# A graph network layer on one core: layer norm's centring on ScalarE and its scale at the split of h, in PSUM

## The chip, the core and the metric

The kernel runs on one core of a Trainium2 chip. TensorE (PE in the profile, its weight loads PEld) multiplies matrices and writes to PSUM. VectorE (DVE) and ScalarE (ACT) work element by element on SBUF and PSUM. GpSimd (POOL) here issues the indirect DMAs that scatter rows to memory, and SyncE's queue (SP) issues the other DMAs. The engines run on their own and wait for each other through semaphores. The metric is the device time of one execution in microseconds.

## What is computed

12,500 nodes with 128 features, 412,500 edges sorted by destination. The reference, cut to what matters:

```python
def ssp(x): return softplus(x) - LOG2
hn  = maximum(layernorm(x), 0)                 # (x - mean) / sqrt(var + 1e-5), then relu
h   = hn @ W_in2f                              # 12500 x 128
Wij = (ssp(f_ij @ W_f1 + b_f1) @ W_f2 + b_f2) * rcut_ij[:, None]
agg = segment_sum(h[dst] * Wij, src, 12500)    # one row an edge
out = x + ssp(agg @ W_o1 + b_o1) @ W_o2 + b_o2
```

Layer norm has no weights. Its scale 1/sqrt(var) is positive, one number a node, so it may be applied before the relu, after it, or after the product with W_in2f: relu(s·c) @ W = s·(relu(c) @ W).

## The kernel before, in words

**Edges.** The edges run in 806 chunks of 512, one chunk a step of the main loop (`for k in range(-3, ...)`, line 1200; `step`, line 989). In a step PE, ACT and DVE work on several chunks in different phases: the filter network (PE `hidden` line 682, ACT Abs, Exp and Ln on lines 691 to 694, DVE line 700, all for two chunks at once every second step, then PE `value` line 797 onto a bias that ACT writes to PSUM, line 789); the gather of h rows (a DMA of a window of h into `near`, a DVE comparison line 776, PE `pick` line 808, ACT `picked` line 818, which multiplies by the edge weight); the row number of each message in its destination table (DVE lines 705 and 729, PE lines 724 and 757); the message itself (DVE line 826). GpSimd then scatters the four 128-row tiles of the message to `slots` (line 830).

**Pace.** `behind` (line 586) ties PE's work of a chunk to the landing of the scatters of eight chunks before, and the message tile `o` has eight buffers.

**Quads of nodes.** h is made by `make_h` (line 327), 512 nodes (a quad, four 128-row tiles) at a time, 25 quads, 98 tiles. It is a generator: each `yield` ends what it emits into one step. The first two quads run ahead of the loop. `side` (line 1158) starts one of the other 23 every nine steps from about step 6 on, so they take about the first 210 of the 806 steps. Counted from a quad's start, these are its ticks:

- 0: the load of x into `xb`; 3: DVE statistics (lines 338, 339), ACT Ln and Exp for the scale `rs` (342, 343)
- 4: DVE four small operations that sharpen `rs` (347 to 351), then DVE centres and scales each tile of `xb` (line 354, four instructions)
- 5: PE transposes to PSUM (359), ACT relu to `xT` (361)
- 6: PE multiplies by W_in2f into the PSUM tile `hps` (365), ACT rounds it to bf16 (367, one instruction)
- 7: DVE subtracts the rounded part into the SBUF tile `left` (370), ACT rounds the rest (371)
- 8: DVE subtracts again (373): h is kept as three bf16 parts. SP stores them to memory (379, 388).

`xps` and `hps` share one PSUM bank (tag `acc`, one buffer). What a step of the loop issues comes ahead of what the quad's tick issues on every engine's queue.

**The output.** x is loaded again for the residual, and the output bias `bo2` (with W_o2's share of b_o1 in it, line 321) is added early: `x_ahead` (line 1092) does this for 14 quads on DVE from step 300 on (`x_early`) and for the other 11 on GpSimd near the end (`x_late`), both through `x_bias` (line 423). `rest` (line 1139) prepares late constants beside the quads and ends with `late_biases`. `count_ps` (line 550) is a PSUM tile with the numbers 0 to 127, which DVE compares with on lines 705 and 882.

Of the kernel before, what the change touches and what calls it, by code (L numbers as in the profile page):

```python
# [9 lines left out]
F32 = mybir.dt.float32  # L10
# [3 lines left out]
AF = mybir.ActivationFunctionType  # L14
ALU = mybir.AluOpType
PSUM = bass.MemoryType.PSUM

P = 128
TG = 16
CH = 512  # L20
NCHUNK = TG * P // CH
QT = CH // P
# [21 lines left out]
def gnn_kernel(  # L44
# [20 lines left out]
    nc = tc.nc  # L65
# [52 lines left out]
    def sbuf(name, shape, dtype=F32):  # L118
        return const.tile(shape, dtype, name=name)

    def spread(t, n):
        return t[:, None, :].to_broadcast([t.shape[0], n, P])
# [13 lines left out]
    for c in range(NC):  # L136
        n = c * CH * N // n_edges
# [6 lines left out]
    bf2, bo2 = (sbuf(n, [P, P]) for n in ("bf2", "bo2"))  # L144
# [20 lines left out]
    ln = ctx.enter_context(tc.tile_pool(name="ln", bufs=2))  # L165
# [150 lines left out]
    def late_biases(psum):  # L316

        nc.vector.tensor_scalar(nbo1, bo1, -1.0, None, op0=ALU.mult)
        b12 = psum.tile([P, QT, P], F32, name="b12_out", tag="acc")[:, 0, :]
        nc.tensor.matmul(b12, bo1.to_broadcast([P, P]), wo2, start=True, stop=True)  # L320
        nc.vector.tensor_add(bo2, b12, bo2)
# [5 lines left out]
    def make_h(q, psum):  # L327

        n = min(QT, NTILE - q * QT)
        xb = early.pop(q, None)  # L330
        if xb is None:
            xb = load_x(q)
            for _ in range(3):
                yield
        st = ln.tile([P, QT, 6], F32, name="st")
        mv = ln.tile([P, QT, 2], F32, name="mv")
        for i in range(n):
            nc.vector.bn_stats(st[:, i, :], xb[:, i, :])
            nc.vector.bn_aggr(mv[:, i, :], st[:, i, :])

        rs = ln.tile([P, QT], F32, name="rs")
        nc.scalar.activation(rs[:, :n], mv[:, :n, 1], AF.Ln, bias=eps)
        nc.scalar.activation(rs[:, :n], rs[:, :n], AF.Exp, scale=-0.5)
        yield

        ve = ln.tile([P, QT], F32, name="ve")
        nc.vector.tensor_scalar(ve[:, :n], mv[:, :n, 1], EPS, -0.5, op0=ALU.add, op1=ALU.mult)
        r2 = ln.tile([P, QT], F32, name="r2")
        nc.vector.tensor_mul(r2[:, :n], rs[:, :n], rs[:, :n])
        nc.vector.tensor_mul(r2[:, :n], r2[:, :n], ve[:, :n])  # L350
        nc.vector.scalar_tensor_tensor(rs[:, :n], r2[:, :n], 1.5, rs[:, :n],
                                       op0=ALU.add, op1=ALU.mult)
        for i in range(n):
            nc.vector.tensor_scalar(xb[:, i, :], xb[:, i, :], mv[:, i, 0:1], rs[:, i:i + 1],
                                    op0=ALU.subtract, op1=ALU.mult)
        yield
        xps = psum.tile([P, QT, P], F32, name="xps", tag="acc")
        for i in range(n):
            nc.tensor.transpose(xps[:, i, :], xb[:, i, :], ident)
        xT = ln.tile([P, QT, P], F32, name="xT")  # L360
        nc.scalar.activation(xT[:, :n, :], xps[:, :n, :], AF.Relu)
        yield
        hps = psum.tile([P, QT, P], F32, name="hps", tag="acc")
        for i in range(n):
            nc.tensor.matmul(hps[:, i, :], xT[:, i, :], win, start=True, stop=True)
        hb = ln.tile([P, QT, 3, P], BF16, name="hb")
        nc.scalar.activation(hb[:, :n, 0, :], hps[:, :n, :], AF.Copy)
        yield
        left = ln.tile([P, QT, P], F32, name="left")
        nc.vector.tensor_sub(left[:, :n, :], hps[:, :n, :], hb[:, :n, 0, :])  # L370
        nc.scalar.activation(hb[:, :n, 1, :], left[:, :n, :], AF.Copy)
        yield
        nc.vector.tensor_sub(hb[:, :n, 2, :], left[:, :n, :], hb[:, :n, 1, :])
        for (b, rows), table in zip(tables, h3_t):
            lo = max(0, b - q * QN) // P
            hi = min(n, (b + rows - q * QN) // P)
            if lo < hi:
                r = q * QN + lo * P - b
                nc.sync.dma_start(
                    table[r:r + (hi - lo) * P, :].rearrange("(c p) f -> p c f", p=P),  # L380
                    hb[:, lo:hi, :, :].rearrange("p c k f -> p c (k f)"))
                if b + rows == QN:
                    yield
            if q == NQ - 1:
                for r in range(NTILE * P - b, rows, P):
                    if r >= 0:
                        nc.sync.dma_start(table[r:r + P, :], none)
        nc.sync.dma_start(
            h3[q * QN:q * QN + n * P, :].rearrange("(c p) f -> p c f", p=P),
            hb[:, :n, :, :].rearrange("p c k f -> p c (k f)"))  # L390
        yield
# [15 lines left out]
    def x_pieces(t0, n):  # L407

        n0 = t0 * P
        full = min(n, N // P - t0)  # L410
        rest = N - n0 - full * P if full < n else 0
        pieces = []
        if full:
            pieces.append((P, slice(0, full), slice(n0, n0 + full * P)))
        if rest:
            pieces.append((rest, slice(full, n), slice(n0 + full * P, N)))
        return pieces
# [2 lines left out]
        for p, cs, rows in pieces:  # L420
            nc.sync.dma_start(xo[:p, cs, :], x[rows, :].rearrange("(c p) f -> p c f", p=p))

    def x_bias(xo, pieces, engine=nc.vector):
        for p, cs, rows in pieces:
            xi = xo[:p, cs, :]
            engine.tensor_add(xi, xi, spread(bo2[:p, :], xi.shape[1]))

    def finish(t0, n, sT, quad, psum, z, xo=None, bank=("v", 3)):

# [108 lines left out]
    with tc.tile_pool(name="edge", bufs=2) as edge, tc.tile_pool(  # L538
        name="quad", bufs=3
# [7 lines left out]
        free_v = free.rearrange("p (t b) -> p t b", b=NBLK)  # L547


        count_ps = state_ps.tile([P, P], F32, name="count_ps")  # L550

        def clear(seg):

# [497 lines left out]
        t0, i = 0, 0  # L1051
        while i < len(segs):

            j = max(range(i, len(segs)), key=lambda j: sum(todo[i:j + 1]) / (due[j] - t0))
            n = sum(todo[i:j + 1])
            for m in range(n):
                zeros.setdefault(t0 + m * (due[j] - t0) // n, []).append(clears.pop(0))
            t0, i = due[j], j + 1
# [5 lines left out]
        while len(rate) < len(at):  # L1064
            n = len(at) - len(rate)
# [13 lines left out]
        i, k = 0, todo[0][0]  # L1079
# [9 lines left out]
                if todo[i - 1][1].ends(todo[i - 1][2]):  # L1089
                    break  # L1090

        def x_ahead(homes, engine):

            pending = []
            for q, xo in homes:
                n = min(QT, NTILE - q * QT)
                pieces = x_pieces(q * QT, n)
                x_load(xo, pieces)
                xs[q] = xo
                pending.append((xo, pieces))  # L1100
                yield
                yield
                if len(pending) > 2:
                    x_bias(*pending.pop(0), engine)
            for w in pending:
                yield
                x_bias(*w, engine)

        def as_quad(t):
            return t.rearrange("p (c f) -> p c f", f=P)  # L1110
# [4 lines left out]
        def early_homes():  # L1115
            for q in range(NX):
                if q < 6:
                    yield q, quad.tile([P, QT, P], F32, name="xo", bufs=6)
                elif q < 12:
                    yield q, ln.tile([P, QT, P], F32, name="xo", tag=("xb", "xT", "left")[q // 2 - 3],  # L1120
                                     bufs=2)
                else:
                    t = ln.tile([P, QT, 3, P], BF16, name="xo", tag="hb", bufs=2)
                    yield q, as_quad(t.rearrange("p c k f -> p (c k f)")[:, :2 * CH].bitcast(F32))

        def late_homes():
            t = None
            for q in range(NX, NQ):
                i = (q - NX) % 2
                if i == 0:  # L1130
                    if q < NX + 8:
                        t = edge.tile([P, NCHUNK, CH], BF16, name="xr", tag="rel", bufs=4)
                        t = t.rearrange("p c e -> p (c e)").bitcast(F32)
                    else:
                        t = edge.tile([P, NB, CH], F32, name="xf", tag="f")
                        t = t.rearrange("p b e -> p (b e)")
                yield q, as_quad(t[:, i * CH:(i + 1) * CH])

        def rest():

            first_load(1)
            part_load(1)
            late_loads()
            yield from bounds(1, nc.vector)
            shift(1)
            for k in range(1, NPART):
                relative(k)
                if k + 1 < NPART:
                    part_load(k + 1)
                yield  # L1150
                yield
                rel_store(k)
                for _ in range(4):
                    yield
            yield from ranges(psum)
            late_biases(psum)

        def side():

# [11 lines left out]
        with tc.manual_schedule():  # L1171
# [23 lines left out]
            bs[0] = groups[0].bias(0)  # L1195
            group(1)
            aside = side()
            x_early = x_ahead(early_homes(), nc.vector)
            x_late = x_ahead(late_homes(), nc.gpsimd)
            for k in range(-3, max(NCH, max(units) + 1)):  # L1200
                for seg, d in zeros.get(k, ()):
                    seg.clears.append(nc.sync.dma_start(*d).ins.name)
# [34 lines left out]
            for q in range(NQ):  # L1237
                n = min(QT, NTILE - q * QT)
# [12 lines left out]
            q = 0  # L1251
# [19 lines left out]
    with tc.If(missed > 0):  # L1271
        with tc.tile_pool(name="any_e", bufs=2) as edge, tc.tile_pool(
            name="any_q", bufs=2
# [51 lines left out]
```

## Time and profile before

| | us |
|---|---|
| median of 4 runs | 5391.92 (5375.06 to 5407.1) |
| the profiled execution | 5360.8, its span 5359.0 |
| DVE busy on line 354 (98 instructions) | 27.6 |
| DVE busy on line 370 / 373 (25 each) | 16.9 / 16.7 |
| ACT busy on line 367 / 371 (25 each) | 14.6 / 15.3 |
| DVE busy on line 426, early additions (14) | 9.5 |
| POOL idle ahead of line 830, whole span | 2109.7 |

A row of the table of groups gives the line, the engine, the operation, output and inputs by the program's names, the shapes and the count, then busy time, the mean of one in ns, and the idle time of the engine just before these instructions with what ended it. "remote" there is a semaphore whose sender the profile can't name; "issue" is a wait for nothing that it shows. The rows of instructions that overlap count the overlap twice in the mean.

### The profile page before, as it was taken

To read this page: it belongs to the slowest core of one execution; us is meant where nothing else is said; L and a number is where in the kernel's file an instruction comes from. 1 tells how busy PE (TensorE), PEld (TensorE's weight loads), DVE (VectorE), ACT (ScalarE), POOL (GpSimd) and SP (SyncE) were. 2 spreads that over 40 slices of the span, in tenths; PEclk is the share of its full clock that TensorE was granted. 3 is DMA by queue.
4 is the path that set the end of the run, shared out by engine and by line. 5 is a ranking of instruction groups with operands and counts; after the bars stand their busy time and mean duration, and the time that the engine had idled before them with its cause. 6 is when DMAs were issued, how large, how long until landed. Compare 5 with 4: busy or idle time off the path is not lost. (4 is left out here: it accounts for less than half of the span.)

```text
span 5359.0 us, 74346 instructions
## 1 busy us (share of the span) xinstructions
PE 3738.0 (70%) x21598; PEld 2866.6 (53%) x21598; DVE 3138.8 (59%) x7101; ACT 2788.0 (52%) x5464; POOL 3148.8 (59%) x3292
## 2 busy tenths in 40 slices
PE   6555655555655555588888888877887777777768
PEld 3343434333433333366666666666666666666657
DVE  5555555555444444466666666666666666666657
ACT  5555555555555555555555555555454554544433
POOL 4666666666666666666666665665565665555552
PEclk8666666666666666688888888888887888888889
DMA  5445444444433334355556555566555655565546
GB/s 150 143 144 148 140 133 141 134 124 134 115 99 99 94 107 143 116 171 180 171 180 214 165 167 166 165 185 197 169 171 156 209 180 147 170 187 152 149 123 190
DMA packets 515221, 820.65 MB, mean 153 GB/s; under 512 B 177188, under 2 KB 312728, under 8 KB 514812
## 3 DMA queue, kind: packets, MB, share of 16 engines
q1 hardware_dynamic: 411212, 602.55, 39.1%
q0 software_dynamic: 103168, 213.15, 11.9%
q8 instruction: 180, 2.95, 0.2%
q14 instruction: 229, 1.88, 0.1%
q10 hardware_dynamic: 432, 0.13, 0.0%
HBM read 419.75 MB, written 395.69 MB: 152 GB/s over the span
## 5 line engine op out<-in xcount | busy, mean ns | idle before, releaser
L830 POOL DMA_INDIRECT slots<-o,slot x3224 | 3111.0, 965 | 2109.7 <-DVE o L826 1228.8
L818 ACT ACTIVATE hg<-picked,rcut 128x128 f32<-128x128 f32 x3224 | 915.2, 366 | 1398.0 <-remote 752.5
L903 PEld LDWEIGHTS acc<-to,m 128*128 128x128 f32 x8152 | 1211.4, 229 | 541.3 <-issue 386.6
L903 PE MATMUL acc<-to,m 128*128 128x128 f32 x8152 | 1320.2, 320 | 254.5 <-issue 165.0
L797 PEld LDWEIGHTS v<-wf,r 128*128 128x128 f32 x6448 | 1090.6, 250 | 389.1 <-issue 262.2
L797 PE MATMUL v<-wf,r 128*128 128x128 f32 x6448 | 1183.5, 340 | 128.4 <-ACT v L789 64.9
L826 DVE TENSOR_TENSOR o<-v,hg 128x512 f32<-128x512 f32 x806 | 553.1, 686 | 1000.2 <-remote 535.4
L682 PE MATMUL z<-f,wf 20*128 20x512 f32 x1612 | 625.1, 854 | 462.5 <-DVE r L700 265.2
L882 DVE TENSOR_TENSOR to<-count_ps,m 128x640 f32<-128x640 f32 (+3 forms) x793 | 637.8, 827 | 294.2 <-remote 114.1
L789 ACT ACTIVATE v<-bf 128x512 f32<-128x512 f32 x804 | 485.0, 603 | 456.7 <-DVE o L826 265.3
L729 DVE TENSOR_REDUCE top<-free 128x4 f32<-128x392 f32 x806 | 449.2, 557 | 457.4 <-remote 309.2
L808 PE MATMUL picked<-near,at 96*128 96x128 bf16 x3224 | 391.3, 256 | 374.5 <-DVE o L826 280.6
L757 PE MATMUL free<-inb,rest_of 128*128 128x392 f16 x806 | 329.7, 409 | 363.6 <-issue 224.8
L700 DVE SCALAR_TENSOR_TENSOR r<-z,nbf,a 128x1024 f32<-128x1024 f32 x403 | 514.2, 1276 | 103.1 <-issue 63.8
L691 ACT ACTIVATE a<-z,bf 128x1024 f32<-128x1024 f32 x403 | 445.9, 1106 | 230.0 <-remote 108.0
L808 PEld LDWEIGHTS <-at 96*128 96x128 bf16 x3224 | 312.1, 118 | 433.8 <-issue 404.9
L682 PEld LDWEIGHTS z<-f,wf 20*128 20x128 f32 x1612 | 156.6, 234 | 672.3 <-DVE r L700 357.8
L694 ACT ACTIVATE a<-a,half 128x1024 f32<-128x1024 f32 x403 | 463.2, 1149 | 13.2
L705 DVE TENSOR_TENSOR inb<-count_ps,blk 128x392 f16<-128x392 f32 x806 | 446.1, 554 | 0.0
L692 ACT ACTIVATE a<-a 128x1024 f32<-128x1024 f32 x403 | 426.3, 1058 | 12.8
L724 PE MATMUL free<-inb,after 128*128 128x392 f16 x806 | 331.3, 411 | 8.2 <-issue 4.4
L724 PEld LDWEIGHTS <-after 128*128 128x128 f16 x806 | 91.5, 114 | 370.7 <-issue 366.5
(115 smaller groups left out, 1428.2 us busy)
## 6 DMA issues: line engine op xcount, KB each, us to landing
m<-slots SPq DMA_DIRECT2D x307, 387.0 KB
m<-slots SPq DMA_DIRECT2D x278, 322.5 KB
rel<-rel_d SPq DMA_DIRECT2D x202, 384.0 KB
slots<-o,slot POOLq DMA_INDIRECT x3224
m<-slots SPq DMA_DIRECT2D x193, 258.0 KB
slots<-zero SPq DMA_DIRECT2D x96, 387.0 KB
f<-in_f_t SPq DMA_DIRECT2D x404, 80.0 KB
slots<-zero SPq DMA_DIRECT2D x58, 516.0 KB
```

The lines of the kernel that those rows point to most:

```text
L682: mm = nc.tensor.matmul(z[:, k, :], wf1[rows, :], self.f[rows, :], start=True, stop=True)
L694: nc.scalar.activation(a, a, AF.Ln, bias=half, scale=0.5)
L700: nc.vector.scalar_tensor_tensor(r, z, nbf1, a, op0=ALU.max, op1=ALU.add)
L729: nc.vector.tensor_reduce(self.top[:, c * QT:(c + 1) * QT], free_v, axis=mybir.AxisListType.X, op=ALU.max)
L789: nc.scalar.activation(v, spread(bf12, QT), AF.Copy)
L797: mm = nc.tensor.matmul(v[:, i, :], r[:, i * P:(i + 1) * P], wf2, start=False, stop=True, skip_group_check=True)
L808: mm = nc.tensor.matmul(ps[:, i, :], at[:, i * P:(i + 1) * P], near, start=i == 0, stop=i == QT - 1, skip_group_check=True)
L818: nc.scalar.activation(hg[:, i, :], ps[:, i, :], AF.Copy, scale=self.rcut[:, j:j + 1])
L826: nc.vector.tensor_mul(o[:, :, :P], v, hg)
L830: put = nc.gpsimd.indirect_dma_start(out=views[j % VIEWS], out_offset=bass.IndirectOffsetOnAxis(ap=self.slot[:, j:j + 1], axis=0), in_=o[: ...
L882: nc.vector.tensor_tensor(to[:, :n, :], count_ps[:, None, :].to_broadcast([P, n, P]), m[:, :n, P:].to_broadcast([P, n, P]), op=ALU.is_equal)
L903: nc.tensor.matmul(self.acc[b // QT][:, i, :], m[:, j, :P], to[:, j, :], start=t == 0, stop=t == self.seg.tiles(b) - 1)
```

## The change

From the third quad on (`q > 1`) four things differ in `make_h`. DVE writes the negated means to a small tile `nm`, and ACT centres each tile of `xb` with an Identity activation whose bias is `nm`; DVE's centring and scaling on line 354 is left out. The product is then without the scale. ACT rounds each tile of `hps` on its own with the scale `rs` as a per-partition operand, four instructions for one. DVE multiplies each tile of `hps` by `rs` and subtracts the rounded part in one instruction, four for one, in place in PSUM. For all quads `left` is gone: the remainder stays in `hps`, and ACT and DVE read it from there.

The PSUM tile of `count_ps` grows to 512 columns and holds a copy of `bo2` beside the numbers, which ACT writes once at the end of `rest`. The early additions of the bias on DVE read that copy; the late ones on GpSimd read `bo2` in SBUF as before.

```diff
         ve = ln.tile([P, QT], F32, name="ve")
+        if q > 1:
+            nm = ln.tile([P, QT], F32, name="nm")
+            nc.vector.tensor_scalar(nm[:, :n], mv[:, :n, 0], -1.0, None, op0=ALU.mult)
+            for i in range(n):
+                nc.scalar.activation(xb[:, i, :], xb[:, i, :], AF.Identity, bias=nm[:, i:i + 1])
         nc.vector.tensor_scalar(ve[:, :n], mv[:, :n, 1], EPS, -0.5, op0=ALU.add, op1=ALU.mult)
...
-        for i in range(n):
+        for i in range(n if q < 2 else 0):
             nc.vector.tensor_scalar(xb[:, i, :], xb[:, i, :], mv[:, i, 0:1], rs[:, i:i + 1],
                                     op0=ALU.subtract, op1=ALU.mult)
...
-        nc.scalar.activation(hb[:, :n, 0, :], hps[:, :n, :], AF.Copy)
+        if q < 2:
+            nc.scalar.activation(hb[:, :n, 0, :], hps[:, :n, :], AF.Copy)
+            yield
+            nc.vector.tensor_sub(hps[:, :n, :], hps[:, :n, :], hb[:, :n, 0, :])
+        else:
+            for i in range(n):
+                nc.scalar.activation(hb[:, i, 0, :], hps[:, i, :], AF.Copy, scale=rs[:, i:i + 1])
+            yield
+            for i in range(n):
+                nc.vector.scalar_tensor_tensor(hps[:, i, :], hps[:, i, :], rs[:, i:i + 1],
+                                               hb[:, i, 0, :], op0=ALU.mult, op1=ALU.subtract)
+        nc.scalar.activation(hb[:, :n, 1, :], hps[:, :n, :], AF.Copy)
         yield
-        left = ln.tile([P, QT, P], F32, name="left")
-        nc.vector.tensor_sub(left[:, :n, :], hps[:, :n, :], hb[:, :n, 0, :])
-        nc.scalar.activation(hb[:, :n, 1, :], left[:, :n, :], AF.Copy)
-        yield
-        nc.vector.tensor_sub(hb[:, :n, 2, :], left[:, :n, :], hb[:, :n, 1, :])
+        nc.vector.tensor_sub(hb[:, :n, 2, :], hps[:, :n, :], hb[:, :n, 1, :])
...
-    def x_bias(xo, pieces, engine=nc.vector):
+    def x_bias(xo, pieces, engine=nc.vector, b=bo2):
...
-            engine.tensor_add(xi, xi, spread(bo2[:p, :], xi.shape[1]))
+            engine.tensor_add(xi, xi, spread(b[:p, :], xi.shape[1]))
...
-        count_ps = state_ps.tile([P, P], F32, name="count_ps")
+        numbers = state_ps.tile([P, CH], F32, name="numbers")
+        count_ps, bo2_ps = numbers[:, :P], numbers[:, P:2 * P]
...
             late_biases(psum)
+            nc.scalar.activation(bo2_ps, bo2, AF.Copy)
...
-            x_early = x_ahead(early_homes(), nc.vector)
-            x_late = x_ahead(late_homes(), nc.gpsimd)
+            x_early = x_ahead(early_homes(), nc.vector, bo2_ps)
+            x_late = x_ahead(late_homes(), nc.gpsimd, bo2)
```

`x_ahead` takes `b` and hands it to `x_bias`.

More of the change, by code (lines that the diff above doesn't have):

```diff
@@ L1090, in gnn_kernel, with x_ahead @@
                     break
-        def x_ahead(homes, engine):
+        def x_ahead(homes, engine, b):
             pending = []
@@ L1103, in x_ahead @@
                 if len(pending) > 2:
-                    x_bias(*pending.pop(0), engine)
+                    x_bias(*pending.pop(0), engine, b)
             for w in pending:
                 yield
-                x_bias(*w, engine)
+                x_bias(*w, engine, b)
         def as_quad(t):
```

## The prediction

> **What bounds the kernel now.** I read the page first, then the engines' busy time by stretches, the waits and the time line of single quads. The page:
>
> ```profile
> span 5359.0 us, 74346 instructions
> PE 3738.0 (70%) x21598; PEld 2866.6 (53%) x21598; DVE 3138.8 (59%) x7101; ACT 2788.0 (52%) x5464; POOL 3148.8 (59%) x3292
> POOL 4666666666666666666666665665565665555552
> ```
>
> No engine is full, and GpSimd is at six tenths from end to end: the kernel is a ring. A chunk's scatters must land before PE works on the chunk eight further on, that work makes a message, and the message starts the next scatters. What the changed part costs is read from stretches: with quads, after them and before the first collection of `slots`, and the long second part.
>
> ```profile
> 150.00:1350.00 1200.00, 679.90 (x3304) 470.79 (x3301) 645.14 (x1737) 670.69 (x1342) 735.35 (x760) 0.66 0.46 138
> 1450.00:1900.00 450.00, 261.22 (x1156) 172.52 (x1156) 202.30 (x481) 243.97 (x471) 280.11 (x292) 0.62 0.34 95
> ```
>
> Columns: stretch, length, busy us (instructions) of PE, PEld, DVE, ACT and POOL, granted clock, DMA share, GB/s. POOL issues four scatters a step: 760/4 = 190 steps in 1200 us, 6.32 us each; 292/4 = 73 in 450 us, 6.16 us. So all that a quad does, nine steps' worth, costs 9 x 0.16 = 1.4 us, and the 23 quads 33 us, though one quad occupies DVE for some 4.9 us (4 x (0.265 + 0.182) statistics, 0.63 small ones, 1.13 line 354, 0.69, 0.68) and ACT for 2.3 (0.29 + 0.21 + 0.59 + 0.59 + 0.62). Over 80% is already absorbed. The waits show by what, from 150 to 1350 us:
>
> ```profile
> POOL slots L830 <- DVE o L826: 254.4, 76, 7.0
> ACT hg L818 <- remote: 166.1, 45, 9.4
> DVE top L729 <- remote: 153.7, 23, 10.6
> DVE o L826 <- remote: 135.8, 28, 11.4
> ```
>
> Columns: total us, times, longest. Every 16 us or so ACT and DVE both stand still for up to 11 us, for a signal whose sender isn't named, and POOL runs dry for a message 76 times. Such a standstill is the cover of everything that the change adds. At its end comes the one place where a quad's own work is first in the queue:
>
> ```profile
> 801.63 0.60 ACT L367 ACTIVATE hb<-hps 128x512 bf16<-128x512 f32 x1 [11.00 <-remote]
> 802.13 1.14 ACT L818 ACTIVATE hg<-picked,rcut 128x128 f32<-128x128 f32 x4
> 802.26 0.69 DVE L370 TENSOR_TENSOR left<-hps,hb 128x512 f32<-128x512 f32 x1 [6.98 <-ACT hb L367]
> 802.87 0.16 DVE L825 COPY o<-place 128x4 f32<-128x4 f32 x1
> 803.30 0.69 DVE L826 TENSOR_TENSOR o<-v,hg 128x512 f32<-128x512 f32 x1 [0.27 <-ACT hg L818]
> ```
>
> ACT's rounding, then ACT's `hg`, then DVE's message: a longer line 367 makes this message later.
>
> **The change, part by part.** From the third quad on there are 22 full quads and one of two tiles: 90 tiles, 23 quads, 22.5 full ones.
>
> *Centring, tick 4.* DVE loses four instructions, 1.13 us back to back, and gains `nm`, a 128x4 tensor_scalar like line 347 (0.16 us): -0.97 us. ACT gains four; the trace has no Identity from SBUF with a bias. The nearest row is line 818, 128x128 with a per-partition operand, four in 1.14 us; the far ends are line 1173 (0.281 alone, no operand, 1.12 for four) and line 342 (0.297 alone for four columns; 128 more cannot take it past line 818's 0.37, 1.5 for four). I take 1.16 us. Of 23 quads, 11 have ACT idle for 2.9 to 7.4 us just after DVE's line 347, where the four lie free. In the other 12 ACT is at `v` or about to start the Abs, Exp, Ln triple, and the triple moves by up to 1.26 us, 15 us in all; there DVE reaches its next message 0.97 us sooner, 12 us. The tick behind these is mostly one of the standstills, so I take 0, with -22 (0.97 x 23) to +15 as ends.
>
> The added wait: ACT stands for `nm` behind DVE's whole step. Behind it on ACT are `hg` (DVE's message waits), the bias `v` (PE's `value` waits) and the log triple (DVE's line 700 waits). Line 342 waits in the same manner one tick earlier, 40.1 us for 25, or 1.6 us. In the 11 quads ACT is idle anyway; in the 12 DVE has passed inb when the triple starts. I take 0; without that cover 23 x 1.6 = 37 us, which goes to a rival.
>
> The Trainium skill speaks against this part. "ScalarE: Activation LUTs", in its rules for kernel authors, sends adds and multiplications to VectorE, and for an ACTIVATE with a pointer bias it gives about 280 ns plus 0.833 ns a column, less 93 ns of overlap, by which four would come to an estimated 1.18 us. DVE's four took 1.13 us here, so rule and row agree on the price and part on whether it lies in ACT's idle time; by the rule alone this part would be a loss of the order of its full length.
>
> *Rounding with the scale, tick 6.* One instruction of 0.59 us becomes four like line 818, which also read PSUM and multiply: 1.14, so +0.55 us. In 17 of the 23 quads ACT comes to it out of a wait, and in all 23 `hg` follows with no gap: 17 x 0.55 = 9 us on the path. Ends 0 (the next standstill takes it) and 23 x 0.75 = 17, where DVE's four also push the message by 0.2.
>
> *Subtraction, tick 7.* DVE's 0.69 becomes four 128x128 ones from PSUM; near rows are line 661 (the same operation in SBUF, 0.296) and line 321 (PSUM input, 0.291): 1.16, so +0.47, between +0.4 and +0.5. It is in the 17 us above; elsewhere DVE waits after it for `hg` 1.6 us or more (line 826's gap in most quads), so 0 more. Line 371 reads PSUM: 0.619 falls to line 367's 0.592, nothing; line 373 stays at 0.68.
>
> *The bank.* `hps` is held until line 373, one tick longer. The next writer of `acc` is the next quad's transposes at tick 14, six ticks on; with that gone PE would stand for a step, 6 us. SP's stores of h keep place and number; `h` is read from memory many steps later. No DMA is added or moved.
>
> *GpSimd's side.* Lines 354, 373 and 426 leave two-operand or fast reads of SBUF. POOL's scatter takes 968 ns on average between 100 and 1450 us and 0.96 us undisturbed, so at most 858 x 0.008 = 7 us were lost to whatever disturbs it, and POOL has idle time. I take -3, ends -7 and 0.
>
> "SBUF — State Buffer", section "Who interferes with whom", in the skill says that a two-port or two-SBUF-input VectorE instruction shuts GpSimd out for its whole length. If each of them did, the removed ones would have cost an estimated 25 + 16 + 10 = 51 us of POOL; the row above shows no such loss.
>
> *Early additions.* 14 of 0.68 us stay 0.68, as lines 926 and 426 do with and without PSUM (0.684, 0.679); at most their 9.5 us are won. ACT's one copy of `bo2` is a line 1173, 0.28 us, plus one wait for DVE's line 321; behind it stands one step's `hg`: between 0 and 2 us, I take 0.
>
> Sum: 0 + 9 + 0 - 3 + 0 = +6 us on the profiled 5360.8. That execution was 31 us under the median of the four, so I add the 6 to 5391.92: **5398 us**. A check from the other side: quads let through 1.4 of 7.2 us; of ACT's +1.7 and DVE's -0.5, a net +1.2, that share is 0.24 us, 5 us for all. Own range: ends -38 (-22, 0, -7, -9) and +34 (15, 17, 0, 2), so 5354 to 5426.
>
> **The rivals.**
>
> *ACT closes the ring* (slower). Place: ticks 4 and 6. Price: (1.16 + 0.55) x 22.5 = 38 us, 5430; with the wait for `nm` uncovered up to 37 more, 5467. For it: after a standstill ACT runs without a gap from 801.6 to 814 us. Against: 11 of 23 quads have ACT idle at tick 4, and over 80% of a quad is absorbed. It decides as soon as the standstill that follows no longer shrinks by what ACT grew, from about 1.2 us a quad.
>
> *DVE and POOL are freed* (faster). Tick 4 is DVE's: steps there that meet no wait take 3.6 us, DVE's own sum. All of 0.97 x 23 = 22, 7 for POOL and 9 for the additions: -38, 5354. Against: DVE has 46% idle in the stretch, tick 7 gives 0.47 back, and all quads together cost 33.
>
> *The activation doesn't come for nothing*: Identity is in no row, and if it lies outside the loaded table, each quad takes two loads of 1.283 us (line 265), 23 x 2.57 = 59 us, 5451. One load for five functions so far speaks against it.
>
> The same "ScalarE: Activation LUTs", section "Table sets: the hidden batching unit", says that identity is in every set; no run here has shown it yet.
>
> **How the numbers follow.** A measurement of this kernel can tell about 0.5%, 27 us, from no change: 5365 to 5419 is "same". The forecast of +6 has 0.58, nearly all of it inside; ACT's ring 0.23; DVE and POOL freed 0.16; the table 0.03. Faster takes 0.16 and 0.02 of the forecast's tail; slower 0.23 + 0.03 less 0.02 that end under 27 us. That gives 0.18, 0.58, 0.24. The range runs from the fast rival's 5354 to a little past ACT's 38 us, as most of that rival's weight is near its lower end: 5354 to 5436.
>
> **What would show it.** Right: line 354 with 8 instructions, ACT's new rows near 0.37 us each as line 818's, one table load; the stretch from 150 to 1350 us within two or three scatters of 760; ACT's busy time there up by some 35 us and its idle time down as much. Slower by ACT: fewer than 752 scatters there, POOL's wait for line 826 grown by 30 us or more, `hg` waiting less for "remote". Faster: over 766 scatters, POOL's mean down to 0.96. Wrong altogether: if the stretches past 1900 us, where only the place of one bias and of `count_ps` differ, move by more than the early part; then the cause lies in the enlarged PSUM tile or in the pace of the scatters, of which I have taken nothing.

## The result, and the profile after

The changed kernel takes 5398.61 us (median of 52 runs, 5379.54 to 5427.65), the kernel before 5393.01 us (78 runs, 5363.94 to 5427.32): ratio 1.0014, 95% interval 1.0005 to 1.0022. The medians differ by 5.6 us, and the ratio makes it some 7; only the number of runs sets so small a loss clear of no change. The profiled execution has a span of 5394.5 us. The head of its page and the groups that answer to those shown of before:

```profile
span 5394.5 us, 74527 instructions
PE 3756.9 (70%) x21598; PEld 2879.3 (53%) x21598; DVE 3135.8 (58%) x7101; ACT 2823.4 (52%) x5622; POOL 3130.6 (58%) x3292
POOL 4655655655666656666666655655555555555552
```

DVE has as many instructions as before, 7101: 90 centrings left out, 23 `nm` and 67 further subtractions added. ACT has 158 more. POOL is busy for 18 us less with the same 3224 scatters, but for 5 us less than in a second profile of the kernel before (3135.6). The stretches that the prediction compared, of the changed kernel (length, busy us and instructions of PE, PEld, DVE, ACT, POOL, then clock, DMA share, GB/s):

```profile
150.00:1350.00 1200.00, 689.84 (x3244) 475.30 (x3245) 631.33 (x1711) 693.52 (x1468) 715.06 (x746) 0.65 0.45 135
1450.00:1900.00 450.00, 255.38 (x1149) 169.58 (x1147) 203.70 (x484) 242.86 (x474) 278.69 (x292) 0.64 0.35 98
2400.00:5000.00 2600.00, 2052.70 (x12970) 1665.18 (x12966) 1648.67 (x3441) 1319.21 (x2584) 1509.47 (x1576) 0.82 0.57 173
```

With quads, 746 scatters for 760 before: 6.43 us a step for 6.32. Without them, 292 for 292. The long second part has 1576; before, it had 1594, though only the place of one bias and of `count_ps` differs there. The kernel before, profiled a second time (span 5401.6 us), shows 755, 289 and 1574. A stretch of one profile is therefore known to about 1%, which is more than the whole effect. Here are the long part of the first profile before, then the early stretch in the second profile of before and of the changed kernel:

```profile
2400.00:5000.00 2600.00, 2068.97 (x13150) 1679.09 (x13150) 1670.62 (x3473) 1333.24 (x2615) 1532.31 (x1594) 0.83 0.58 175
150.00:1350.00 1200.00, 683.52 (x3279) 475.92 (x3280) 644.18 (x1729) 665.91 (x1336) 727.43 (x755) 0.65 0.46 138
150.00:1350.00 1200.00, 701.95 (x3254) 485.19 (x3254) 633.15 (x1717) 697.07 (x1474) 717.58 (x748) 0.65 0.45 136
```

With both profiles of each kernel (746 and 748 after, 760 and 755 before) the early stretch still stands apart, the others don't. As a size this can't be used: 10 scatters are 2.6 steps or some 17 us, more than the whole loss.

The new instructions, in the table of groups from 150 to 1350 us (busy us, mean ns, then the idle time ahead and what ended it):

```profile
L351 ACT ACTIVATE xb<-xb,nm 128x128 f32<-128x128 f32 x84 | 26.6, 387 | 38.8 <-DVE nm L349 25.7 <-DVE r L713 7.5 <-DMA near<-h 5.7
L378 ACT ACTIVATE hb<-hps,rs 128x128 bf16<-128x128 f32 x84 | 23.8, 365 | 103.5 <-remote 99.1 <-DMA slots<-zero 3.3 <-PE hps L370 1.0
...
L342 ACT ACTIVATE rs<-mv,eps 128x4 f32<-128x4 f32 x21 | 6.1, 290 | 27.1 <-issue 14.7 <-DVE mv L339 10.6 <-DVE st L338 1.8
```

```profile
L381 DVE SCALAR_TENSOR_TENSOR hps<-hps,rs,hb 128x128 f32<-128x128 f32 x84 | 30.1, 358 | 61.0 <-ACT hb L378 56.3 <-issue 2.4
...
L349 DVE TENSOR_SCALAR nm<-mv 128x4 f32<-128x4 f32 x21 | 3.3, 156 | 0.0
```

84 instructions are 21 full quads. Four centrings take 26.6 / 21 = 1.27 us, four roundings 23.8 / 21 = 1.13 us, four subtractions 30.1 / 21 = 1.43 us: the four of DVE don't overlap (4 x 358 ns is 1.43 us), ACT's do. ACT now stands for `nm` ahead of the centring, 25.7 us in all here and 11.5 us in the second profile of the changed kernel. What was already a wait of ACT for a signal without a named sender ahead of line 367 is now ahead of line 378.

### The profile page after: what moved, and what is told of

Its sections match the earlier page's. It is cut to its first block, busy times and chain, and to the rows that moved or that the text cites. A ratio compares the mean times of both kernels' runs of the same rounds, so it can differ in the third digit from the quotient of the medians.

```text
span 5394.5 us, 74527 instructions
## 1 busy us (share of the span) xinstructions
PE 3756.9 (70%) x21598; PEld 2879.3 (53%) x21598; DVE 3135.8 (58%) x7101; ACT 2823.4 (52%) x5622; POOL 3130.6 (58%) x3292
## 5 line engine op out<-in xcount | busy, mean ns | idle before, releaser
L895 DVE TENSOR_TENSOR to<-numbers,m 128x640 f32<-128x640 f32 (+3 forms) x793 | 638.0, 828 | 313.7 <-remote 138.8
L718 DVE TENSOR_TENSOR inb<-numbers,blk 128x392 f16<-128x392 f32 x806 | 446.1, 554 | 0.0
```

The lines of the kernel that those rows point to most:

```text
L895: nc.vector.tensor_tensor(to[:, :n, :], count_ps[:, None, :].to_broadcast([P, n, P]), m[:, :n, P:].to_broadcast([P, n, P]), op=ALU.is_equal)
```

## The experiments

The twelve runs met three chips of two kinds, and that became the main finding. In what follows *chip A* stands for the kind where the kernel before takes about 5390 us, as in the result above and in the second four runs, and *chip B* for the kind where the same kernel takes about 4233 us: one chip in the first four runs, another in the last four. Each run is compared with runs of the kernel before on its own chip.

### First four: the parts (chip B; before 4233.59 us)

**The early bias from PSUM alone**, on the kernel before:

```diff
...
+        numbers = state_ps.tile([P, CH], F32, name="numbers")
+        count_ps, bo2_ps = numbers[:, :P], numbers[:, P:2 * P]
...
+            nc.scalar.activation(bo2_ps, bo2, AF.Copy)
...
+            x_early = x_ahead(early_homes(), nc.vector, bo2_ps)
```

> The kernel before with the last part of the change alone: the enlarged PSUM tile, the copy of bo2 and the early additions from it. Theory A (the loss comes from the four roundings with a scale at tick 6, 0.55 us of ACT a quad just ahead of hg): no difference, ratio 0.999 to 1.001. Theory B (the loss comes from the centring on ACT and its wait for nm): the same. Theory C (the loss comes from the PSUM tile or the bias): ratio about 1.0014, some 8 us more.

Measured: 4227.77 us, ratio 0.9989 (0.9980 to 0.9998). A small gain, which no theory had.

**Centring back on DVE**, on the changed kernel:

```diff
-            nm = ln.tile([P, QT], F32, name="nm")
-            nc.vector.tensor_scalar(nm[:, :n], mv[:, :n, 0], -1.0, None, op0=ALU.mult)
             for i in range(n):
-                nc.scalar.activation(xb[:, i, :], xb[:, i, :], AF.Identity, bias=nm[:, i:i + 1])
+                nc.vector.tensor_scalar(xb[:, i, :], xb[:, i, :], mv[:, i, 0:1], None,
+                                        op0=ALU.subtract)
```

> The changed kernel with the centring back on DVE (four subtractions, no nm), the scale still applied at the split. Theory A: the loss stays, ratio 1.001 to 1.002, because the four roundings stay. Theory B: the loss goes, ratio 0.998 to 1.0005, since ACT loses 1.2 us a quad and the wait.

Measured: 4227.80 us, 0.9986 (0.9977 to 0.9995).

**ACT centres and scales, the split whole**, on the changed kernel:

```diff
... (the changed kernel's nm and centring, ahead of the chain for rs, are taken out)
+        if q > 1:
+            nm = ln.tile([P, QT], F32, name="nm")
+            nc.vector.scalar_tensor_tensor(nm[:, :n], mv[:, :n, 0], -1.0, rs[:, :n],
+                                           op0=ALU.mult, op1=ALU.mult)
+            for i in range(n):
+                nc.scalar.activation(xb[:, i, :], xb[:, i, :], AF.Identity,
+                                     scale=rs[:, i:i + 1], bias=nm[:, i:i + 1])
...
-        if q < 2:
+        if q < NQ:
             nc.scalar.activation(hb[:, :n, 0, :], hps[:, :n, :], AF.Copy)
```

> The changed kernel with ACT both centring and scaling x (bias -mean*rs, scale rs, behind DVE's chain for rs) and with the split as it was, one rounding and one subtraction a quad, in PSUM. Theory A: the loss goes, ratio 0.9995 to 1.0005. Theory B: it stays or grows, ratio 1.0015 to 1.004, because ACT now also waits for the 0.6 us chain.

Measured: 4224.72 us, 0.9978 (0.9969 to 0.9987).

**`nm` a tick earlier**, on the changed kernel:

```diff
+        nm = ln.tile([P, QT], F32, name="nm")
+        if q > 1:
+            nc.vector.tensor_scalar(nm[:, :n], mv[:, :n, 0], -1.0, None, op0=ALU.mult)
         rs = ln.tile([P, QT], F32, name="rs")
...
-            nm = ln.tile([P, QT], F32, name="nm")
-            nc.vector.tensor_scalar(nm[:, :n], mv[:, :n, 0], -1.0, None, op0=ALU.mult)
```

> The changed kernel with nm computed one tick earlier, right behind the statistics, so that ACT's centring finds it ready. Theory A: as the changed kernel, ratio 1.0005 to 1.002; ACT's idle time before the centring (38.8 us from 150 to 1350 us) goes and comes back elsewhere. Theory B, if it is the wait: ratio 0.999 to 1.0005.

Measured: 4225.28 us, 0.9979 (0.9970 to 0.9988).

All four are gains here, so none of them tells theory A from B: the loss that they were to locate did not appear on this chip. The question became why the sign differs (theory D in what was written before the next runs).

### Second four: the two kernels again, and doses at tick 4 (chip A; before 5381.19 us)

> The kernel before again, for its profile beside the others' on the same chip. The four runs so far met a chip on which the kernel before takes 4233.6 us, not 5393, and there all four variants took 0.9978 to 0.9989 of it. Theory D (the late completions of PE, 45% of the span in the first profile, cover or stretch what the change moves, and without them the change is a gain): on a chip at 4230 us hardly any late completion of PE, quads from step 15 to 222 in 1030 to 1036 us. Theory A: the same profile, but the quads no slower than in the four variants.

> The changed kernel again. Theory D: on a chip at about 4230 us ratio 0.997 to 0.999, on one at about 5390 us 1.0005 to 1.002. Theory A (ACT's four roundings cost wherever it runs): 1.000 to 1.002 on either.

Measured: before, one run, 5403.3 us; the changed kernel 5392.85 us, ratio 1.0025 (1.0004 to 1.0046). A loss on chip A, a second time. What theory D says of a chip at 4230 us was not tested by these two.

**Three times the centring on ACT**, in the changed kernel; the scratch tile is used for nothing:

```diff
+            more = ln.tile([P, QT, P], F32, name="more", tag="left")
+            for i in range(2 * n):
+                nc.scalar.activation(more[:, i % n, :], xb[:, i % n, :], AF.Identity,
+                                     bias=nm[:, i % n:i % n + 1])
```

> The changed kernel with eight more ACT instructions a full quad behind the centring, into a scratch tile: three times the centring, 2.3 us of ACT a quad, 52 us in all. If ACT closes the ring in these ticks: 30 to 52 us more than the changed kernel. If the standstills take it up: at most 10 us more on a chip at 5390 us; on one at 4230 us, where ACT is 70% busy in this stretch, 10 to 30 us more.

Measured: 5390.55 us, 1.0033 (1.0013 to 1.0053), beside 5392.85 of the changed kernel. The dose is there in the profile and costs nothing that can be told (group of 150 to 1350 us):

```profile
L354 ACT ACTIVATE more<-xb,nm 128x128 f32<-128x128 f32 x168 | 51.0, 385 | 0.0
```

51 us of ACT in 21 quads, and the stretch has 746 scatters, as many as the changed kernel's. This much ACT time at tick 4 is covered on chip A.

**Eight more instructions on DVE where line 354 stood**, in the changed kernel:

```diff
+        if q > 1:
+            more = ln.tile([P, QT, P], F32, name="more", tag="left")
+            for i in range(2 * n):
+                nc.vector.tensor_scalar(more[:, i % n, :], wf2, mv[:, i % n, 0:1],
+                                        rs[:, i % n:i % n + 1], op0=ALU.subtract, op1=ALU.mult)
```

> The changed kernel with eight more DVE instructions a full quad where line 354 stood, of its kind (from a constant in SBUF to a scratch tile): twice what the change took off DVE at tick 4, 2.3 us a quad, 52 us in all. If DVE is what the change relieved: 20 to 50 us more than the changed kernel on a chip at 4230 us, at most 10 us on one at 5390 us. If DVE's time there is free: within 5 us of the changed kernel on both.

Measured: 5401.80 us, 1.0049 (1.0029 to 1.0068). 46.7 us of DVE from 150 to 1350 us cost some 9 us; the interval overlaps the changed kernel's, so a cost is likely and not shown. By these 9 us, what the change can have won by taking less than half of that time off DVE's tick 4 is some 4 us.

### Last four: doses at ticks 6 and 7, and a version without the moves to ACT (chip B; before 4232.05 us)

> The changed kernel once more, as the base of the three others on their chip. Where the kernel before takes about 5390 us: ratio 1.0005 to 1.0025 as in the two measurements so far; where it takes about 4230 us: theory A 1.000 to 1.002, theory D (a gain where PE's completions are not late) 0.997 to 0.999.

Measured: the changed kernel 4223.05 us, 0.9979 (0.9970 to 0.9988). Theory D's number: on chip B the change is a gain of 9 us. That the late signals are what turns the sign is not shown by it.

**Three times the rounding at tick 6**, ahead of `hg`:

```diff
+            more = ln.tile([P, QT, P], F32, name="more", tag="left")
+            for i in range(2 * n):
+                nc.scalar.activation(more[:, i % n, :], hps[:, i % n, :], AF.Copy,
+                                     scale=rs[:, i % n:i % n + 1])
```

> The changed kernel with eight more roundings a full quad at tick 6 into a scratch tile, just ahead of hg: 2.3 us of ACT a quad, 52 us in all, the same amount as the dose at tick 4, which cost nothing that could be told (ratio 1.0033 beside 1.0025). Theory A (ACT's time counts at tick 6, as it leads the queue out of a standstill): 20 to 45 us more than the changed kernel. Rival (a quad's ACT time counts nowhere): at most 8 us more.

Measured: 4222.93 us, 0.9979 (0.9970 to 0.9988). The rival's number, but on chip B; whether it costs on chip A was not tried.

**Three times the subtraction at tick 7**:

```diff
+            more = ln.tile([P, QT, P], F32, name="more", tag="left")
+            for i in range(2 * n):
+                nc.vector.scalar_tensor_tensor(more[:, i % n, :], hps[:, i % n, :],
+                                               rs[:, i % n:i % n + 1], hb[:, i % n, 0, :],
+                                               op0=ALU.mult, op1=ALU.subtract)
```

> The changed kernel with eight more multiply-and-subtract instructions a full quad on DVE at tick 7, ahead of its own four: 2.3 us of DVE a quad ahead of the message, 52 us in all, five times what the change added there. If DVE at tick 7 is where the change loses: 20 to 45 us more than the changed kernel, which makes its +0.47 us a quad 4 to 9 us. If not: at most 8 us more.

Measured: 4222.98 us, 0.9981 (0.9972 to 0.9990). Free on chip B as well.

**The remainder and the bias in PSUM, nothing moved to ACT**, on the kernel before:

```diff
-        left = ln.tile([P, QT, P], F32, name="left")
-        nc.vector.tensor_sub(left[:, :n, :], hps[:, :n, :], hb[:, :n, 0, :])
+        nc.vector.tensor_sub(hps[:, :n, :], hps[:, :n, :], hb[:, :n, 0, :])
... (the next rounding and the last subtraction read hps in place of left; the bias in PSUM as above)
+            x_early = x_ahead(early_homes(), nc.vector, bo2_ps)
```

> The kernel before with the parts of the change that move no work to ACT: the remainder in PSUM for all quads and the early bias from PSUM; line 354 and the one rounding and one subtraction a quad stay as they were. Theory A: no loss, ratio 0.999 to 1.0005 where the kernel before takes 5390 us, and there a gain over the changed kernel of 0.1 to 0.2%. If the loss sits in hps being held a tick longer or in the PSUM tile: 1.001 to 1.002.

Measured: 4223.09 us, 0.9979 (0.9970 to 0.9988). The whole gain of chip B comes without moving anything to ACT. This version beats the kernel before there and ties with the changed one; on chip A it was not run.

## Why the sign differs

On chip B no engine stands for a signal without a named sender, and POOL doesn't starve. The waits of the changed kernel on chip B, 150 to 1120 us:

```profile
DVE o L838 <- DMA slots<-o,slot: 258.5, 121, 7.0
POOL slots L843 <- issue: 174.4, 572, 0.3
PEld z L695 <- DVE r L713: 171.5, 95, 3.3
```

And the same kernel on chip A, 150 to 1350 us:

```profile
POOL slots L843 <- DVE o L839: 278.2, 80, 7.4
POOL slots L843 <- issue: 201.6, 655, 1.5
DVE top L742 <- remote: 141.2, 21, 11.2
ACT hg L831 <- remote: 101.9, 24, 6.4
DVE o L839 <- remote: 100.6, 18, 8.8
ACT hb L378 <- remote: 82.6, 10, 10.9
```

On chip B messages wait for their buffer, that is for scatters to land, and POOL has 0.3 us between two scatters and no longer wait: it is the bound. 950 scatters in 1200 us are 1.263 us each, its 0.96 and 0.30. On chip A POOL waits for messages for 278 us. So on chip B, where the 0.30 stays, only a shorter scatter can pay. It is shorter: POOL's group from 100 to 1120 us, with the early bias alone changed (first fence), with the whole change and with nothing moved to ACT (second), the first on one chip B and the others on another:

```profile
L831 POOL DMA_INDIRECT slots<-o,slot x804 | 776.3, 966 | 245.2 <-issue 182.7 <-DMA slots<-o,slot 28.4 <-DVE at L777 8.8
```

```profile
L843 POOL DMA_INDIRECT slots<-o,slot x807 | 774.8, 960 | 246.1 <-issue 183.3 <-DMA slots<-o,slot 25.6 <-DVE at L789 11.3
L830 POOL DMA_INDIRECT slots<-o,slot x807 | 774.8, 960 | 246.1 <-issue 183.9 <-DMA slots<-o,slot 23.5 <-DVE at L776 8.2
```

6 ns on 805 scatters are 4.8 us, and the ratios 0.9989 and 0.9979 are some 4 us apart, with intervals that overlap. On the first chip B alone, the two variants that centre on ACT (961 ns) took 3.0 and 2.5 us less than the early bias alone; the one that centres on DVE (962 ns) took as long as it, which the scatters don't explain. The version with nothing moved to ACT has 960 ns with line 354 still on DVE; so what shortens the scatter is the remainder's move to PSUM. The trace of the early bias alone tells which line it is. Line 370 (output `left`, one input in PSUM) and line 373 (both inputs in SBUF), each beside a scatter:

```profile
664.14 0.68 DVE L370 TENSOR_TENSOR left<-hps,hb 128x512 f32<-128x512 f32 x1
664.14 0.96 POOL L831 DMA_INDIRECT slots<-o,slot  x1 [0.30 <-issue]
666.62 0.68 DVE L373 TENSOR_TENSOR hb<-left,hb 128x512 bf16<-128x512 f32 x1
666.67 1.46 POOL L831 DMA_INDIRECT slots<-o,slot  x1 [0.30 <-issue]
```

Of the 29 scatters that overlap with line 370 none takes over 0.97 us; of the 29 that overlap with line 373, 12 do, by 3.9 us together; line 354 accounts for 0.3 us. The other part of the gain, 0.9989, belongs to the bias. The kernel before wasn't profiled on chip B, but the traces of chip A show the cause, in the kernel before and in the changed one, from 1955 to 2110 us, where the 14 additions run:

```profile
L830 POOL DMA_INDIRECT slots<-o,slot x103 | 103.8, 1008 | 52.1 <-issue 27.1 <-DVE o L826 22.9 <-DMA slots<-o,slot 0.9
```

```profile
L843 POOL DMA_INDIRECT slots<-o,slot x101 | 96.8, 959 | 59.4 <-DVE o L839 29.8 <-issue 29.7
```

A scatter there took 1008 ns (978 in the second profile of before) while DVE added with two inputs from SBUF, and 959 with one in PSUM: 2 to 5 us in all (101 x 0.019, 103 x 0.049). On chip A it buys nothing that can be seen: the stretch holds 103 and 101 scatters before and 101 and 102 after, and POOL's idle time in it is 52.1 and 57.0 us before, 59.4 and 58.5 after.

The Trainium skill has the rule behind this in "SBUF — State Buffer", section "Who interferes with whom": a VectorE instruction with two SBUF inputs contends with a GpSimd instruction that reads SBUF. The rows agree, 1008 and 978 ns against 959. Blocked for their whole length, the 14 additions of 0.68 us would have cost POOL 9.5 us; 2 to 5 were seen. Single scatters of the first profile show why:

```profile
2005.41 1.66 POOL L830 DMA_INDIRECT slots<-o,slot  x1 [0.30 <-issue]
2005.55 0.68 DVE L426 TENSOR_TENSOR xo<-xo,bo 128x512 f32<-128x512 f32 x1
2012.57 0.96 POOL L830 DMA_INDIRECT slots<-o,slot  x1 [0.30 <-issue]
2012.82 0.68 DVE L426 TENSOR_TENSOR xo<-xo,bo 128x512 f32<-128x512 f32 x1
```

An addition that starts 0.14 us after the scatter lengthens it by 0.70 us; one that starts 0.25 us after it leaves it as it is. It holds in the two traces of the kernel before and the one of the early bias alone: an instruction of line 373 or 426 that already ran when a scatter began, and went on for 0.15 us or more, held it in 37 of 38 cases, as if the scatter stood from 0.12 us after its start until that instruction's end; of 67 that began 0.2 us or more after the scatter's start, one lengthened it. That the scatter reads SBUF just then is inferred.

## Why the prediction was right, and where it wasn't

**The time** (5398, measured 5398.61) and the side are right, and the likeliest case, no change beyond 0.5%, is what came. That the number fits to a microsecond is luck: terms of a few us, some of them off, add up to 6, the term that makes it a loss, +9 at tick 6, is not shown by any run, and the profile can't show an effect of 7 us in 5390.

**The absorption** was the main step, and at tick 4 it is confirmed on chip A: 51 us more of ACT cost nothing that can be told there, and 46.7 us more of DVE some 9 us, if anything. At ticks 6 and 7 it was tried on chip B alone, where 44.9 and 44.2 us (150 to 1120 us) cost nothing either. The rival "ACT closes the ring" expected 38 us from 1.7 us a quad, and fell; "DVE and POOL are freed" fell on chip A; on chip B its POOL half is the right mechanism, and its DVE half adds nothing, as the version that leaves line 354 on DVE gains as much. The table of activations was not loaded again: one load, as before.

**Centring: 0.** Its price was 1.27 us a quad for 1.16; that so much ACT time is free on chip A the dose shows. The estimate of 1.18 us in the prediction takes the overlap off four times; four instructions in a row overlap three times, and with the same figures that gives the 1.27 us measured.

**Rounding at tick 6: +9.** The price is right (0.54 us for 0.55). That it is what the change loses on chip A is argued and not shown: the dose at tick 6 met chip B, where nothing of this kind costs. The loss on chip A, 1.0014 and 1.0025 in two measurements, has four candidates left: tick 6 on ACT, tick 7 on DVE, ACT's wait for `nm` (25.7 and 11.5 us in the two profiles), which the prediction put at 0, and the bank that `hps` holds a tick longer. Their experiments met chip B, so this stays open.

**Subtraction at tick 7** was mis-sized: +0.74 us a quad (1.43 less 0.69), not +0.47. The near rows, 0.296 and 0.291 us for one, were too short for this instruction, which multiplies and subtracts from PSUM into PSUM: one takes 0.358 us.

**GpSimd: -3, ends -7 and 0.** Right for the quads as time of POOL: the lengthened scatters beside line 373 add up to 2.9 and 2.5 us in the two profiles of chip A and 3.9 us on chip B. It left out line 426, whose 14 instructions add 4.2 and 2.5 us, about twice as much for each, because the 968 ns were read up to 1450 us, ahead of the additions. I had costed the early additions by DVE's time alone, 0.68 against 0.68.

**What would show it**: "fewer than 752 scatters" was to mean a loss by ACT. It came (746, 748), but POOL's wait for messages grew by 25 and 11 us, short of the 30 that were asked for, and the dose then showed that ACT at tick 4 isn't the cause. The sign of being right, two or three scatters around 760, was narrower than the noise of a profile: the kernel before itself gave 755 the second time. The last test, that the late stretch should move less than the early one, failed as a test: two profiles of one kernel differ there by 20 scatters in 1594.

## What to carry to other kernels

Before a change of a few us is priced, ask which engine's queue is never empty. On chip B, where that was GpSimd, only the shorter scatter paid, and 44 us more on ACT or DVE cost nothing. The same change was a gain of 0.2% there and a loss of 0.1 to 0.25% where GpSimd starved. Take two-input SBUF operations of VectorE out of GpSimd's way by keeping one operand in PSUM when it is there anyway; on chip B that alone was all of the gain.

## What the runs showed of the hardware that had not been expected

The same program takes about 5390 us on chip A and 4233 us on chip B, with the same instructions and nearly the same durations on ACT, DVE and POOL: a scatter takes 0.96 us on both. PE's matmuls of line 916 take 320 ns on the one and 298 on the other. On chip A, ACT and DVE wait for signals that the profile can't attribute, for up to 11 us at a time (166.1, 153.7 and 135.8 us in the three longest such rows of the first profile, partly at once); in none of the eight traces of chip B does the list of waits have such a row. In the first trace's records of semaphores these waits end when several signals of PE arrive together, at 801.6 to 801.8 us for matmuls recorded before 795.2. The stretches from the end of a PE instruction to PE's next signal, where they exceed 1.5 us, cover 46 to 49% of the span in the six traces of chip A, and at most 0.5% in the eight of chip B. What delays them on chip A is open, and so is whether they are the cause of the loss there; no run tells. The granted TensorE clock differs as well, 0.75 and 0.83 over the span, which may be a result of the standstills or a cause.
